# The first batch of a fused four-layer kernel in plain fp32: its products without splits, its small weights kept raw

## The chip, the cores and the metric

The kernel runs on one core of a Trainium2 chip. Its engines work side by side, each through its own queue in order: TensorE (PE, with its weight loads PEld), VectorE (DVE), ScalarE (ACT), GpSimd (POOL), and SyncE (SP), which issues transfers. The metric is the device time of one execution in microseconds; lower is better. Three executions of the kernel before took 2854.42, 2855.34 and 2858.27 us: the median is 2855.34.

## The reference

Sixteen sequences (batches) of 256 positions by 256 features go through four layers, each added to its input:

```
x = x + L0(x)     # traces: 16 decaying sums per sequence, gated, then layernorm
x = x + L1(x)     # masked softmax pooling over the sequence
x = x + L2(x)     # 8 experts and a shared one, 256 -> 1024 -> 256, all of them, weighted
x = x + L3(x)     # 256 -> 1024 -> 256, a part of the output weights chosen per sequence
```

What the change touches is L0 and L1 of the first sequence. In short:

```
ctx = scan(x, decay_ctx)
h1  = gelu(x @ Wn1);  mod = 0.5 + sigmoid(h1 @ Wn2)          # 16 rows, one per decay
g   = x * sigmoid([x, ctx] @ Wg)
temporal = sum over d of blend[d] * scan(g * mod[d], decay[d])
out = (gelu(x @ Wsoma) * sigmoid(temporal @ Wtemp)) @ Wout;  x1 = x + layernorm(out)
s   = tanh(x1 @ W1) @ v;  p = softmax(mask(s));  x2 = x1 + (p @ x1) / count
```

## The kernel before, in words

[...] So the kernel splits each operand in a rounded and a low part: `rnd` (L86) makes the rounded one, mostly on ScalarE (L88), `low` (L94) subtracts it from the original on VectorE or GpSimd (L95), and `mm3` (L100) makes a product of three passes: L101 high by high, L102 high by low, L103 low by high. Weights are split too: the small ones of L0 and L1 into `wh` and `wl` (`split_small`, L130), the expert weights chunk by chunk into a ring of ten tiles (`load_chunk`, L523), from two raw buffers. A raw buffer is free for the next transfer when both halves of its split are done.

Two generators give the work of one batch in steps: `traces(b, fast)` (L247) for the front of L0 and the decay loop, `pooled(b, fast)` (L392) for the rest of L0 and for L1. `fast` is true for batch 0 alone, which has nothing to hide behind: it uses two PSUM banks for most of its products, works in halves, and in its decay loop broadcasts the modulation by TensorE (L330), scales it on ScalarE (L335), multiplies on GpSimd (L338), scans on VectorE (L341), and sums with the identity on TensorE (L344). That last product is in plain fp32. The other batches send their modulation through DRAM and broadcast it by DMA (L354).

The order comes from the program's text, from a scheduler that fills each engine's queue by its own estimate of times, and from `tc.issue_after(...)`, which holds instructions behind a given one. First the constants are loaded (L137 to L154, on SP's and ScalarE's queues) and worked out (L160 to L224). Then 13 steps of batch 0's traces run (`FIRST`, L803), then pooled of batch 0 mixed with the first `FRONT` = 4 steps of batch 1's traces (L759), and the first expert chunks are fetched meanwhile (`prefetch`). From then on a plan of expert units (`l2_unit`, L620: products pg, pu, then y) and last-layer units (`l3_chunk`, L663) runs on TensorE, and the steps of batches 1 to 15 are spread between them at a pace set by due times.

Of the kernel before, what the change touches and what calls it, by code (L numbers as in the profile page):

```python
# [8 lines left out]
F32 = mybir.dt.float32  # L9
F32R = mybir.dt.float32r  # L10
# [6 lines left out]
NB = 16  # L17
# [6 lines left out]
FRONT = 4  # L24
SLACK = 16
# [19 lines left out]
def fused_kernel(  # L45
# [77 lines left out]
    small = {}  # L123

    def load_small(c0, c1, tag):
        raw = l0.tile([P, 512], F32, tag=tag, name=f"raw_{c0}", bufs=L0_BUFS.get(tag, 1))
        nc.sync.dma_start(raw[:, : c1 - c0], wsmall[:, c0:c1])
        small[c0] = raw[:, : c1 - c0]

    def split_small(c0, e):  # L130
        raw = small.pop(c0)
        c1 = c0 + raw.shape[1]
        rnd("a", wh[:, c0:c1], raw)
        low(e, wl[:, c0:c1], raw, wh[:, c0:c1])
# [4 lines left out]
    load_small(O_N1, O_N1 + 256, "bt")  # L139
    bl = const([P, 2, ND], F32, "bl", blend)  # L140
    load_small(O_G, O_G + 512, "tr")
    vec = const([P, V_COLS], F32, "vec", vecs)
    pti = const([P, NB], I32, "pti", ptype.partition_broadcast(P))
    sgt = const([P, NB], F32, "sgt", sgate.partition_broadcast(P))
    gat = const([P, NB, NE], F32, "gat", gates.partition_broadcast(P))
    load_small(O_G + 512, O_G + 1024, "tr")
    load_small(O_SO, O_SO + 512, "xo")
    load_small(O_TE, O_TE + 512, "sc")
    load_small(O_OU, O_OU + 512, "x1")
    load_small(O_W1, O_W1 + 256, "mb")  # L150
# [3 lines left out]
    eix = const([1, NB], I32, "eix", eidx, nc.sync)  # L154
    coef = cp.tile([P, NB, NE + 1], F32, name="coef")
# [7 lines left out]
    V.reciprocal(alpha, alpha)  # L163

    decay = ps_l.tile([P, ND + 1], F32, tag="decay", name="decay")
    V.tensor_copy(decay, alpha)
# [13 lines left out]
    vr = cp.tile([P, 2], F32R, name="vr")  # L180
    V.tensor_copy(vr[:, 0:1], vec[:, V_V : V_V + 1])
    low("v", vr[:, 1:2], vec[:, V_V : V_V + 1], vr[:, 0:1])
    n2 = cp.tile([P, 2, 48], F32R, name="n2")
    V.tensor_copy(n2[:, 0, :], vec[:, V_WN2 : V_WN2 + 48])
    low("v", n2[:, 1, :], vec[:, V_WN2 : V_WN2 + 48], n2[:, 0, :])

# [3 lines left out]

    jrow = cp.tile([P, 2], I32, name="jrow")
    G.iota(jrow, [[P, 2]], base=1, channel_multiplier=1)
    cnt = cp.tile([P, 3, 2], F32, name="cnt")
    V.tensor_copy(cnt[:, 0], jrow)
    V.tensor_scalar(cnt[:, 1], cnt[:, 0], -1.0, S + 1.0, ALU.mult, ALU.add)
    V.memset(cnt[:, 2], S - 1.0)
    flag = cp.tile([P, 3, NB], F32, name="flag")
    ptf = cp.tile([P, NB], F32, name="ptf")
    V.tensor_copy(ptf, pti)
    V.tensor_scalar(flag[:, 0], ptf, 0.0, None, ALU.is_equal)  # L200
    V.tensor_scalar(flag[:, 1], ptf, 1.0, None, ALU.is_equal)
    V.tensor_tensor(flag[:, 2], flag[:, 0], flag[:, 1], ALU.add)
    V.tensor_scalar(flag[:, 2], flag[:, 2], -1.0, 1.0, ALU.mult, ALU.add)

    kindf = cp.tile([P, NB], F32, name="kindf")
    V.tensor_scalar(kindf, flag[:, 0], -2.0, 2.0, ALU.mult, ALU.add)
    V.tensor_tensor(kindf, kindf, flag[:, 1], ALU.subtract)
    kind_i = cp.tile([P, NB], I32, name="kind_i")
    V.tensor_copy(kind_i, kindf)
    cntb = cp.tile([P, NB, 2], F32, name="cntb")  # L210
    ctmp = cp.tile([P, NB, 2], F32, name="ctmp")
    for t in range(3):
        o = cntb if t == 0 else ctmp
        V.tensor_tensor(
            o,
            flag[:, t].unsqueeze(2).to_broadcast([P, NB, 2]),
            cnt[:, t].unsqueeze(1).to_broadcast([P, NB, 2]),
            ALU.mult,
        )
        if t:  # L220
            V.tensor_tensor(cntb, cntb, ctmp, ALU.add)
    mhalf = cp.tile([P, 2], F32, name="mhalf")
    G.memset(mhalf, -0.5)
    bias3 = cp.tile([P, NB], F32, name="bias3")  # L224

# [21 lines left out]
    def traces(b, fast):  # L247
# [3 lines left out]
        rnd("v" if fast else "a", xh, xr)  # L251
        low("v" if fast else "g", xl, xr, xh)
        cx = ft("ta", f"ctx{b}")
        for c in range(2):
            last_of["cx"] = V.tensor_tensor_scan(
                cx[:, c], decay[:, ND : ND + 1].to_broadcast([P, S]), xr[:, c], 0.0, ALU.mult, ALU.add
            )
        yield
        if fast:
            split_small(O_N1, "v")  # L260
# [8 lines left out]
        if fast:  # L269
            with tc.issue_after(last_of["cx"].ins):  # L270
                split_small(O_G, "v")
                split_small(O_G + 512, "v")

                V.tensor_copy(coef[:, :, NE], sgt)
                V.tensor_scalar(sgt, sgt, -1.0, 1.0, ALU.mult, ALU.add)
                V.tensor_tensor(coef[:, :, 0:NE], gat, sgt.unsqueeze(2).to_broadcast([P, NB, NE]), ALU.mult)
# [12 lines left out]
        if fast:  # L289
            ms = l0.tile([48, S], F32R, tag="ths", name=f"ms{b}")  # L290
            rnd("v", ms, md)
            low("v", ms[32:], md[32:], ms[32:])
        else:
            mdd = dram.tile([1, ND, S], F32, tag="mdd", name=f"mdd{b}")
            nc.sync.dma_start(mdd[0], md[0:ND])
        yield
        pg = banks(fast, f"pg{b}")

        ga = ft("ga", f"ga{b}") if fast else ps_a.tile([P, 2, S], F32, tag="ga", name=f"gp{b}")
        for m in range(2):  # L300
            for k in range(4):
                o = O_G + k * S + m * P
                xa, xb_ = (xh[:, k], xl[:, k]) if k < 2 else (ch[:, k - 2], cl[:, k - 2])
                mm3(pg(m), W(0, o, P), W(1, o, P), xa, xb_, k == 0, k == 3)
        for m in range(2):
            A.activation(ga[:, m], pg(m), AF.Tanh, bias=hb[:, V_BG + m : V_BG + m + 1], scale=0.5)
        for c in halves(fast):
            V.scalar_tensor_tensor(ga[:, c], ga[:, c], 1.0, xr[:, c], ALU.add, ALU.mult)
# [12 lines left out]
        if fast:  # L321
            split_small(O_SO, "g")
            split_small(O_TE, "g")

            tacc = ps_y.tile([P, 2, S], F32, tag="y0", name=f"ta{b}")
            for d in range(ND):
                if d % 2 == 0:
                    pb = ps_gu.tile([P, 2, S], F32, tag="gu", name=f"pb{b}_{d}")
                    for i in range(2):
                        PE.matmul(  # L330
                            pb[:, i], sel[:, d + i : d + i + 1].to_broadcast([48, P]), ms, start=True, stop=True
                        )
                mod = l0.tile([P, 2, S], F32, tag="mod", name=f"mod{b}_{d}", bufs=2)
                for c in range(2):
                    last_of["a"] = A.activation(mod[:, c], pb[:, d % 2], AF.Copy, scale=bl[:, c, d : d + 1])  # L335
                bt = ft("bt", f"bt{b}_{d}", 3)
                e = "g" if d else "v"
                last_of[e] = (V if e == "v" else G).tensor_tensor(bt, ga, mod, ALU.mult)  # L338
                tr = ft("tr", f"tr{b}_{d}", 3)
                for c in range(2):  # L340
                    V.tensor_tensor_scan(  # L341
                        tr[:, c], decay[:, d : d + 1].to_broadcast([P, S]), bt[:, c], 0.0, ALU.mult, ALU.add
                    )
                PE.matmul(tacc, ident, tr, start=d == 0, stop=d == ND - 1)  # L344
                if d == 5:
                    soma()
                if d % 2:
                    yield
        else:
            tacc = ft("ta", f"ta{b}")  # L350
            for d in range(ND):
                if d % 2 == 0:
                    mod = l0.tile([P, 2, S], F32, tag="mod", name=f"mod{b}_{d}", bufs=2)
                    nc.sync.dma_start(mod, mdd[0, d : d + 2].partition_broadcast(P))  # L354
                bt = ft("bt", f"bt{b}_{d}", 3)
                tr = tacc if d == 0 else ft("tr", f"tr{b}_{d}", 3)
                with tc.issue_after(last_of[0].ins) if b == 1 and "h" not in last_of else nullcontext():
                    for c in range(2):
                        V.scalar_tensor_tensor(
                            bt[:, c], ga[:, c], bl[:, c, d : d + 1], mod[:, d % 2], ALU.mult, ALU.mult  # L360
                        )
                for c in range(2):
                    V.tensor_tensor_scan(  # L363
                        tr[:, c], decay[:, d : d + 1].to_broadcast([P, S]), bt[:, c], 0.0, ALU.mult, ALU.add
                    )
                if d:
                    G.tensor_tensor(tacc, tacc, tr, ALU.add)  # L367
                if d == 5:
                    soma()
                yield  # L370
# [602 lines left out]
```

## Time and profile before

One profiled execution of the kernel before:

| what | value |
|---|---|
| profiled execution's own time | 2854.52 us |
| its span on the core | 2852.3 us |
| mean granted TensorE clock | 0.993 |
| PE busy (matmuls) | 2781.6 us, 98% of the span |
| DVE busy | 1442.2 us, 51% |
| ACT busy | 1239.2 us, 43% |
| POOL busy | 1295.4 us, 45% |
| PE busy from 0 to 10 us | 1.89 us |
| PE busy from 50 to 60 us | 5.04 us |
| PE busy from 200 to 400 us | 179.09 us |
| PE busy from 400 to 800 us | 398.74 us |

The span is what the profiler saw on the core; the execution's own time also has what lies around it. Busy shares are averages over the whole span, and the first 73 us are of another kind than the rest. The ends of matmuls are modelled, so a busy PE isn't PE at its peak. In rows of the timeline the first two numbers are start and duration in us; the brackets hold the idle time before, and what ended it.

### The profile page before, as it was taken

What the parts mean: (1) busy time and instruction counts of PE and PEld (TensorE: products, weight loads), DVE (VectorE), ACT (ScalarE), POOL (GpSimd) and SP (SyncE); (2) the same over time, 40 slices, a digit from 0 to 9 for tenths busy, and PEclk for the clock granted to TensorE, in tenths of its full rate; (3) what the DMA queues carried; (4) which work ended last, traced back from release to release, by engine and by line L of the source; (5) the groups of instructions that cost most, each with busy time, mean ns of one, the idle gap of its engine ahead of it and who ended that gap; (6) DMA issues with size and microseconds to landing.
All of it is one profiled execution on the core that took longest, in us unless ns stands there. A gap on an engine that the chain in (4) does not pass through costs nothing. (4 is left out here: it accounts for less than half of the span.)

```text
span 2852.3 us, 36958 instructions
## 1 busy us (share of the span) xinstructions
PE 2781.6 (98%) x13632; PEld 2339.8 (82%) x13632; DVE 1442.2 (51%) x2661; ACT 1239.2 (43%) x2054; POOL 1295.4 (45%) x984
## 2 busy tenths in 40 slices
PE   6889889999999999999999999999999999999999
PEld 4887778888888888888888888888888888888887
DVE  7978866665665454444544445444444542222222
ACT  5565544456444533435334443344433453233433
POOL 4755544544645453543534445344454443333333
PEclk8999999999999999999999999999999999999999
DMA  3444546547443532323433143332523242222552
GB/s 106 132 144 137 162 149 217 176 144 244 149 159 120 172 123 100 118 80 92 173 105 125 40 167 117 107 118 66 181 100 110 93 159 98 89 89 76 189 196 86
DMA packets 114694, 371.24 MB, mean 130 GB/s; under 512 B 12642, under 2 KB 30930, under 8 KB 114514
## 3 DMA queue, kind: packets, MB, share of 16 engines
q1 hardware_dynamic: 113650, 368.74, 39.0%
q8 instruction: 108, 1.77, 0.3%
q14 instruction: 72, 0.59, 0.1%
q10 hardware_dynamic: 864, 0.14, 0.0%
HBM read 304.62 MB, written 64.21 MB: 129 GB/s over the span
## 5 line engine op out<-in xcount | busy, mean ns | idle before, releaser
L95 POOL TENSOR_TENSOR hh<-h,hh 128x512 fp32r<-128x512 f32 x640 | 848.4, 1326 | 1327.1 <-ACT hh L88 1307.4
L608 DVE TENSOR_TENSOR h<-h,pu 128x512 f32<-128x512 f32 x576 | 393.9, 684 | 939.6 <-PE pu L103 818.1
L88 ACT ACTIVATE hh<-h 128x512 fp32r<-128x512 f32 x640 | 403.5, 631 | 932.6 <-DVE h L608 912.4
L101 PE MATMUL pg<-x,w_e 128*128 128x512 f32 (+1 forms) x1232 | 467.3, 379 | 12.7 <-ACT x L88 5.4
L607 ACT ACTIVATE h<-pg 128x512 f32<-128x512 f32 x576 | 342.9, 595 | 306.6 <-PE pg L103 228.5
L101 PE MATMUL pu<-x,w_e 128*128 128x512 f32 (+1 forms) x1232 | 465.4, 378 | 6.5 <-ACT h L607 3.7
L103 PE MATMUL pg<-x,w_e 128*128 128x512 f32 (+1 forms) x1232 | 465.7, 378 | 4.2 <-DVE w_e L95 3.4
L102 PE MATMUL y<-hh,w_e 128*128 128x512 f32 (+1 forms) x1232 | 464.4, 377 | 3.2 <-POOL hh L95 3.2
L102 PE MATMUL pg<-x,w_e 128*128 128x512 f32 (+1 forms) x1232 | 465.3, 378 | 0.0
L103 PE MATMUL pu<-x,w_e 128*128 128x512 f32 (+1 forms) x1232 | 463.8, 376 | 0.0
L102 PE MATMUL pu<-x,w_e 128*128 128x512 f32 (+1 forms) x1232 | 463.6, 376 | 0.0
L103 PE MATMUL y<-hh,w_e 128*128 128x512 f32 (+1 forms) x1232 | 463.5, 377 | 0.0
L101 PE MATMUL y<-hh,w_e 128*128 128x512 f32 (+1 forms) x1232 | 415.6, 377 | 1.0 <-DVE acc L655 0.8
L367 POOL TENSOR_TENSOR ta<-ta,tr 128x512 f32<-128x512 f32 x225 | 308.4, 1371 | 67.6 <-DVE tr L363 53.9
L363 DVE TENSOR_TENSOR_SCAN tr<-decay,bt 128x256 f32<-128x256 f32 x450 | 285.1, 672 | 0.0
L101 PEld LDWEIGHTS pg<-x,w_e 128*128 128x128 f32 x1232 | 232.5, 189 | 56.4 <-ACT w_e L88 6.4
L101 PEld LDWEIGHTS pu<-x,w_e 128*128 128x128 f32 x1232 | 232.1, 188 | 50.5 <-ACT h L607 5.8
L103 PEld LDWEIGHTS pg<-x,w_e 128*128 128x128 f32 x1232 | 232.7, 189 | 47.8 <-DVE w_e L95 5.2
L102 PEld LDWEIGHTS y<-hh,w_e 128*128 128x128 f32 x1232 | 233.0, 189 | 47.0 <-POOL hh L95 5.5
L101 PEld LDWEIGHTS y<-hh,w_e 128*128 128x128 f32 x1232 | 231.5, 189 | 44.8 <-ACT hh L88 1.3
L103 PEld LDWEIGHTS y<-hh,w_e 128*128 128x128 f32 x1232 | 233.0, 189 | 41.7
L103 PEld LDWEIGHTS pu<-x,w_e 128*128 128x128 f32 x1232 | 232.3, 189 | 41.9
(294 smaller groups left out, 3267.5 us busy)
## 6 DMA issues: line engine op xcount, KB each, us to landing
w_e<-keep_e SPq DMA_DIRECT2D x216, 768.0 KB, 4.4
raw_e<-in_wexp_dram SPq DMA_DIRECT2D x144, 384.0 KB, 4.5
keep_e<-w_e SPq DMA_DIRECT2D x72, 768.0 KB, 4.2
mod<-mdd SPq DMA_DIRECT2D x120, 256.0 KB, 3.5
w_f<-keep_f SPq DMA_DIRECT2D x56, 384.0 KB, 3.6
raw_c<-in_comb_dram SPq DMA_DIRECT2D x32, 260.0 KB, 2.8
xr<-in_xT_dram SPq DMA_DIRECT2D x16, 256.0 KB, 3.1
xt<-in_x_dram SPq DMA_DIRECT2D x16, 256.0 KB, 2.7
```

The source lines that it names most:

```text
L88: last_of["ca"] = A.activation(out_, in_, AF.Copy)
L95: i = (V if e == "v" else G).tensor_tensor(out_, in_, h.bitcast(F32), ALU.subtract)
L101: PE.matmul(o, wh, xh, start=start, stop=False, **kw)
L102: PE.matmul(o, wh, xl, start=False, stop=False, **kw)
L103: last_of["pe"] = PE.matmul(o, wl, xh, start=False, stop=stop, **kw)
L363: V.tensor_tensor_scan(tr[:, c], decay[:, d : d + 1].to_broadcast([P, S]), bt[:, c], 0.0, ALU.mult, ALU.add)
L367: G.tensor_tensor(tacc, tacc, tr, ALU.add)
L607: A.activation(h, ps_g, AF.Silu)
L608: last_of["h"] = V.tensor_tensor(h, h, ps_u, ALU.mult)
```

## The change

Batch 0 gets generators of its own, `first_traces` and `first_pooled`; `traces` and `pooled` lose their `fast` branches. In the new ones every product but the broadcast of the modulation takes its operands as they are, in fp32, as one `PE.matmul` in place of `mm3`: no operand of batch 0 is rounded and no low part is made. Results in PSUM are brought to SBUF by `evict`, first half on ScalarE, second half on VectorE. The gate products of x (k = 0, 1) are issued ahead of those of ctx (k = 2, 3), soma's products come inside the decay loop, and soma's result `sm` lies in PSUM.

The small weights of batch 0 stay raw in two borrowed tiles (`raw_a` from the pool of x2, `raw_b` from that of acc). The splits, which the other batches need, come later in the text: three groups after the 13 steps with their low part on GpSimd, four by the table `rest` in batch 1's decay loop. In the instruction order that the scheduler makes of it, those four stand early again: on ScalarE between hg and md of batch 0, on GpSimd ahead of the decay loop; the three stand behind the decay loop, ahead of the first two expert chunks.

ScalarE's queue issues only the decays, the blend and the vectors; the types, the shared gate and the gates go to SP's queue. The reciprocal of the decays is written to PSUM at once. The constants that only later steps need are worked out after the first scans (`later_constants`, inside the hold of cx), the coefficients after batch 0 (`coefs`). The steps of batch 1 that are mixed with pooled of batch 0 are `FRONT0` = 3 instead of 4: the gate products of batch 1 come behind.

```diff
+FRONT0 = 3
...
+    raw_a = xs.tile([P, 2048], F32, tag="x2", name="small_a")
+    raw_b = accp.tile([P, 1024], F32, tag="acc", name="small_b")
...
+    def load_small(c0, c1):
+        nc.sync.dma_start(small(c0, c1 - c0), wsmall[:, c0:c1])
...
-    pti = const([P, NB], I32, "pti", ptype.partition_broadcast(P))
-    sgt = const([P, NB], F32, "sgt", sgate.partition_broadcast(P))
-    gat = const([P, NB, NE], F32, "gat", gates.partition_broadcast(P))
...
+    pti = const([P, NB], I32, "pti", ptype.partition_broadcast(P), nc.sync)
...
+    sgt = const([P, NB], F32, "sgt", sgate.partition_broadcast(P), nc.sync)
+    gat = const([P, NB, NE], F32, "gat", gates.partition_broadcast(P), nc.sync)
...
-    V.reciprocal(alpha, alpha)
...
-    V.tensor_copy(decay, alpha)
+    V.reciprocal(decay, alpha)
...
+    rest = {1: (O_SO, 512), 6: (O_TE, 512), 9: (O_OU, 512), 12: (O_W1, 256)}
...
+            if b == 1 and d in rest:
+                split_small(*rest[d], "g")
...
+    def evict(c, o, i):
+
+        if c == 0:
+            last_of["ca"] = A.activation(o, i, AF.Copy)
+        else:
+            last_of["cv"] = V.tensor_copy(o, i)
+
+    def first_traces():
...
+        for k in range(2):
+            PE.matmul(ph[:, :S], small(O_N1 + k * P, P), xr[:, k], start=k == 0, stop=k == 1)
...
+        gates_of((0, 1))
+        yield
...
+        last_of["pm"] = PE.matmul(pm[:48, :S], vec[0:64, V_WN2 : V_WN2 + 48], hg[0:64], start=True, stop=True)
...
+        with tc.issue_after(last_of["pm"].ins):
+            gates_of((2, 3))
...
+        sm = ps_a.tile([P, 2, S], F32, tag="ga", name="sm0")
...
+    def first_pooled():
...
+                PE.matmul(pt[m], small(O_TE + k * S + m * P, P), tt[:, k], start=k == 0, stop=k == 1)
...
+        for c in range(2):
+            last_of["cv"] = V.scalar_tensor_tensor(sg[:, c], sg[:, c], 1.0, sm[:, c], ALU.add, ALU.mult)
...
+        x1T = ft("xo", "x1T0")
+        for c in range(2):
+            evict(c, x1T[:, c], ptr[c])
...
+        q = ft("bt", "q0", 3)
+        for l in range(2):
+            evict(l, q[:, l], ppt[l])
...
+            front = FRONT if b else FRONT0
...
     while n_steps[0] < FIRST:
         next(steps)
+        if n_steps[0] == 4:
+            with tc.issue_after(last_of["cx"].ins):
+                later_constants()
+    with tc.issue_after(last_of["a"].ins), tc.issue_after(last_of["g"].ins), tc.issue_after(last_of["tr"].ins):
+        for off, n in ((O_N1, 256), (O_G, 512), (O_G + 512, 512)):
+            split_small(off, n, "g")
         prefetch(2, 0)
...
     with tc.issue_after(last_of["ca"].ins), tc.issue_after(last_of["cv"].ins):
+        coefs()
         prefetch(RING - n)
```

## The prediction

> **What bounds the kernel now.** I read the busy row in 40 slices first, then a table of stretches, then each engine's timeline up to the first matmul of the expert stage.
>
> ```profile
> PE   6889889999999999999999999999999999999999
> ...
> 30.00:40.00 10.00, 9.79 (x23) 3.64 (x23) 10.00 (x18) 7.27 (x18) 10.00 (x9) 1.00 0.00 1
> ...
> 60.00:70.00 10.00, 6.47 (x32) 5.66 (x30) 5.18 (x15) 4.44 (x10) 1.50 (x1) 0.59 0.58 189
> ...
> 100.00:110.00 10.00, 8.21 (x54) 7.80 (x53) 10.00 (x21) 3.85 (x6) 9.87 (x7) 0.83 0.50 144
> ...
> 800.00:1600.00 800.00, 800.00 (x3788) 671.61 (x3788) 401.83 (x771) 336.47 (x558) 371.30 (x289) 1.00 0.36 122
> ```
>
> The columns after a stretch are its length and the busy time of PE, PE's weight loads, DVE, ACT and POOL. From 400 us on TensorE never rests: nothing there can be won by a shorter wait. The gap is at the front. From 30 to 40 us POOL and DVE are full and PE does bookkeeping; from 60 to 70 us no engine is full: that is one batch going from engine to engine. Then, at 100 us, DVE and POOL are full again, with batch 1's traces and the splitting of expert weights.
>
> ```profile
> 8.11 0.58 PE L101 MATMUL ph<-x,wh 128*128 128x256 f32 x1 [8.11 <-DVE kindf L207]
> ...
> 48.05 0.58 PE L427 MATMUL po0g<-wh,s 128*128 128x256 f32 x1 [2.44 <-ACT s L88]
> ...
> 55.12 0.47 PE L447 MATMUL ptr0g<-ident,x 128*128 128x128 f32 x1 [3.43 <-DVE x L441]
> ...
> 62.25 0.55 PE L467 MATMUL psc<-ths,vr 128*128 128x256 f32 x1 [1.93 <-DVE ths L95]
> ...
> 68.70 0.27 PE L493 MATMUL ppt0g<-ident,sc 128*128 128x128 f32 x1
> ...
> 72.81 0.38 PE L101 MATMUL pg<-x,w_e 128*128 128x256 f32 x1 [0.73 <-ACT x L88]
> ```
>
> Each row is start, duration, operation, and in brackets the idle time before and who ended it. The first expert matmul is at 72.81 us. Everything the change touches lies before that, so the question is how far that row moves, and how much is still there at 400 us.
>
> **Until the trace loop.** Batch 0's loop over 16 decays is POOL's:
>
> ```profile
> 22.14 18.44 POOL L338 TENSOR_TENSOR bt<-ga,mod 128x512 f32<-128x512 f32 x15 [4.97 <-ACT mod L335]
> ...
> 6.12 1.28 ACT L161 ACT_TABLE_LOAD   x1 [6.12 <-DMA bl<-in_blend_dram]
> ...
> 12.05 0.63 ACT L88 ACTIVATE wh<-raw 128x512 fp32r<-128x512 f32 x1 [2.43 <-DMA raw<-in_wsmall_dram]
> ...
> 27.93 0.19 PEld L344 LDWEIGHTS ta<-tr,ident 128*128 128x128 f32 x1 [0.24 <-issue]
> 28.36 0.19 PEld L344 LDWEIGHTS ta<-tr,ident 128*128 128x128 f32 x1 [0.24 <-issue]
> ```
>
> Its 15 products take 18.44 us, 1.23 each, and are not changed; what counts is when the first starts (22.14). In the changed program's order:
> - ScalarE issues three DMAs, so its table load runs at about 2.1 to 3.4 instead of 6.12 behind two more issues. taub lands at 4.9 (0.74 + 4.2), bl at 5.5. DVE's order is reduce, subtract, alpha, reciprocal, reduce, scan: at 0.17 to 0.26 each the scans (0.69 + 0.61) run from 6.4 to 7.7; before, from 9.35 to 11.6. Some twenty index constants follow them, 0.1 each, done by 10.
> - TensorE needs no split: it starts at 5.9, when the first weights land (1.20 + 4.6). An fp32 product is not in this stage before, but the nearest row is: L344 multiplies 512 fp32 columns, has 32 records for 16 calls, and its loads follow 0.43 apart. So 512 columns cost 0.86 and 256 cost 0.43 warm, 0.85 cold, against 0.12 warm and 0.21 cold for one pass of the split form (the pitch of its rows at 18.3 and at 9.0: after a pause TensorE runs at half pace, and rows here come to 0.12 some 3 to 5 us into work). ph takes 5.9 to 7.6; four gate products take 2.9 (cold, warm from about 10) to 10.5; pm to 10.9; the last four to 12.6.
> - The four splits of the other small weights now stand in ScalarE's queue **between hg and md0**. They wait for landings: the third weight group's at 12.05 before, the last at 13.4 (issued 6.90, 6.5 to landing). So md0, whose operand is ready at 10.9, and both ga behind it wait: md0 13.3 to 13.8, ga to 14.6. Nothing hides this; if those landings come early (gates and sgate no longer ahead on ScalarE's queue), md0 is at 11.1.
> - md, ms and its low part on DVE (0.28, 0.28, 0.41), ga (0.85), then pb, mod (0.84), bt (0.69), mod again: POOL's first product at 17.1. POOL's own four low parts (1.28 each, the last half) end at 15.9. Here a rule speaks against the change: by the Trainium skill's "SBUF — State Buffer", section "SBUF: two separate sides", VectorE and GpSimd share a port pair as a lock and the loser waits out the whole instruction. The trace agrees (a cast at 60.30 took 1.35 beside a POOL product, the one at 18.35, as wide, 0.28). By the rule md and ms wait up to 1.3; by unblocked rows nothing. I take 0.5: start at 17.6.
> - Soma now sits after three mod steps: four fp32 products cold (3.4, from 16.2) and two activations hold mod 3 to about 20.4 and POOL some 0.9.
> Sum: 22.14 − 17.6 − 0.9 = **3.6 us** earlier at the loop's end; with bounds 2 (every lock lost) and 7 (landings early).
>
> **From the loop's end to the expert stage**, on the old clock, loop end at 40.58.
> - Five splits on the path go (round on ScalarE, low part on DVE, of t, s, u, ths and q). Where a PSUM tile must still be moved, one copy comes, half on each engine (0.38, 0.42).
> - t ready at 43.95 (before 44.8); four fp32 products, warm: 45.3; the gate's activations to 45.85.
> - The DVE product with soma, in halves:
>
> ```profile
> 45.92 1.63 DVE L413 SCALAR_TENSOR_TENSOR g<-g,sm 128x256 f32<-128x256 f32 x1
> ```
>
> This half took 1.63, the other 0.41: POOL was splitting. With sm in PSUM I take 0.45 each: done at 46.4. po is four products at 0.43, to 47.7; before 51.3.
>
> - POOL is a new bound here. Behind the loop stand now xt + beta (1.28), three weight lows (0.65, 1.28, 1.28), two expert chunks (1.78 each) and batch 1's x (1.25), then the power rs: 40.58 + 9.3 = 49.9, plus 0.7 for itself. DVE has rs ready at 49.2, so 0.7 is lost. x1 at 51.5; before 55.46: 3.9 won.
> - The same POOL queue holds the two raw buffers, so expert chunks 2 and 3 are requested at 46.9 and 48.7 instead of 42.4 and 44.1, and land 3.8 later. Their roundings sit in ScalarE's queue ahead of the copy of x1T: it is done at 54.1 though ptr was at 52.2. pa (two fp32, cold, 1.7), tanh, psc (0.85), reduction: 57.6, before 63.21.
> - Exponential and normalisation as before: 60.05 (before 65.70). The transposes no longer wait for batch 1's 24 gate products (64.04 to 68.84), which go behind the expert stage's start: 60.7. q's copies stand behind chunks 4 and 5: 62.3. pp cold: 64.9. First expert matmul **65.1**, before 72.81: 7.7 won. Bounds: 4 (all of ScalarE's and DVE's copies behind one more chunk, 3.5) and 9.
>
> By a second rule, the skill's "FP8 and Floating Point Precision", section "TensorE Precision Notes", true fp32 takes four passes where the split form takes three. The row says the same of 512 columns (0.86 against 0.235), and 30 products then cost 30 x 0.07 = 2.1 us more warm, 30 x 0.21 = 6.3 cold. By the rule alone this change loses; the waits ahead of the products in the rows above (2.44, 3.43, 1.93) are larger, and I have priced every product in fp32.
>
> **Behind 72.81.** Batch 1's 24 products (0.12 each, 2.9 us), its ga (0.69 on DVE) and the coefficient products (0.5 to 1.7) now come after the start; its trace begins some 3 us later against the expert stage. TensorE idles 3.0 us in the waits at 99.29 (1.23), 103.47 (1.29) and 104.48 (0.50), behind weight splits, so the 2.9 can go there; but DVE is full from 80 to 110 and passes on what it is given. Between 0 and 4 lost; I take 2. The later order, unit by unit, is the same with batch 1's steps about one unit later. The added splits' DMAs are the same transfers.
>
> Sum: 3.6 + 7.7 − 2.0 = **9.3 us**. The profiled execution took 2854.52 (span 2852.3), 0.8 below the median of 2855.34; so 2845.2 by its own time and **2846** as median.
>
> **Rivals.**
> - *Landings come early.* md0 at 11.1 wins 2.5 more, no lock lost, and the 2.9 disappears in idle: 13 to 16, 2841. For: gates' 64 KB leave the front. Against: nothing shows that they delayed the third group.
> - *Supply takes the wait's place.* The expert stage starts early but the chunks, requested 4.6 later on the loop's clock, and the full DVE decide at 100 us; of 11.3 only 2 to 5 are left: 2852, within 0.2% (5.7 us, what a measurement of this kernel can tell from no change). For: ScalarE waits 17.6 us for expert DMAs between 73 and 140. Against: chunks 6 and 7 keep their distance from the start (3.5 us after it, before 3.8).
> - *Slower: fp32 weight loads lie open.* If each record of the 26 fp32 products on the path also pays its load (0.19 warm, 0.33 cold), twice, at the cold clock, the path grows by 26 x 0.66 = 17 us, so 8 lost: 2863. It decides from 0.36 per product; slower by 0.2% needs 0.58. Against: L344's loads (0.19) fit inside 0.43.
> - *The change doesn't do what it says*: the built order has no split on batch 0's path, so no chance for it.
>
> **Numbers.** Forecast 0.50 (its own range 2842 to 2850), early landings 0.20, supply 0.19, open loads 0.11. Faster by over 0.2%: 0.70; within: 0.20; slower: 0.10. Range 2837 to 2860, which takes in the bounds.
>
> **What would show it.** First expert matmul at 59 to 64 us; POOL's loop from 17 to 19; ScalarE idle before a split ahead of md0; power rs waiting on POOL; fp32 records 0.43 apart warm. Wrong if the expert stage starts early and TensorE's waits between 73 and 200 (some 14 us) grow as much.

## The result and the profile after

The changed kernel takes 2841.99 us (median of six executions, 2841.67 to 2842.82); beside it the kernel before took 2854.88 (six, 2852.84 to 2858.44). The ratio is 0.9953, 95% interval 0.9941 to 0.9965: about 12.9 us faster by the medians, 0.47% by the ratio. The spans of the two profiled executions say 12.1: 2852.3 before, 2840.2 after, at nearly the same mean granted clock (0.993 and 0.994).

The same four stretches of the kernel after (columns: length, then busy time and instruction count of PE, PE's weight loads, DVE, ACT, POOL, then the granted clock, the DMA share and GB/s):

```profile
30.00:40.00 10.00, 8.89 (x21) 3.22 (x20) 6.75 (x12) 6.12 (x13) 10.00 (x10) 1.00 0.01 2
60.00:70.00 10.00, 10.00 (x86) 10.00 (x86) 5.72 (x9) 6.47 (x11) 5.13 (x3) 1.00 0.50 159
100.00:110.00 10.00, 8.72 (x68) 8.10 (x67) 10.00 (x20) 4.88 (x7) 9.84 (x7) 1.00 0.35 107
800.00:1600.00 800.00, 799.54 (x3778) 670.31 (x3778) 400.07 (x771) 335.80 (x559) 370.06 (x288) 1.00 0.35 116
```

From 60 to 70 us PE is now full at a clock of 1.00, where it was busy 6.47 of 10 at 0.59: the expert stage has begun. From 800 to 1600 us PE is as full as it was (799.5 of 800, before 800.0). At 100 us DVE and POOL are full as they were.

TensorE's timeline of the kernel after: the rows that answer to those of before, and the ends of what stands ahead of two of them:

```profile
5.93 2.05 PE L488 MATMUL ph<-xr,small_a 128*128 128x256 f32 x4 [5.93 <-DMA small_a<-in_wsmall_dram]
...
40.56 0.70 PE L583 MATMUL po0g<-small_b,g 128*128 128x256 f32 x2 [0.59 <-DVE g L574]
...
41.96 0.59 PE L583 MATMUL po0u<-small_b,g 128*128 128x256 f32 x2
...
45.52 0.33 PE L602 MATMUL ptr0g<-ident,x 128*128 128x128 f32 x1 [0.47 <-DVE x L594]
...
47.40 2.11 PE L609 MATMUL pa<-x1T,small_a 128*128 128x256 f32 x4 [1.04 <-ACT x1T L474]
...
50.07 1.22 PE L614 MATMUL psc<-th,vec 64*128 64x256 f32 x2 [0.56 <-ACT th L611]
...
53.24 0.48 PE L636 MATMUL ppt0g<-ident,sc 128*128 128x128 f32 x1 [0.42 <-DVE sc L631]
...
58.90 0.38 PE L102 MATMUL pg<-x,w_e 128*128 128x256 f32 x1 [0.53 <-ACT x L89]
```

The first expert matmul is at 58.90 instead of 72.81: **13.9 us earlier**, of which 12.1 are left at the end of the profiled execution.

The brackets alone mislead here: they count only the idle time since the instruction just before, and products of batch 1 stand in some of these stretches. What batch 0 waits is the time from the end of one of its products to the start of the next. For that, the last products of po, pa and psc in the kernel before:

```profile
50.99 0.34 PE L429 MATMUL po0u<-wh,s 128*128 128x256 f32 x1
...
57.97 0.42 PE L103 MATMUL pa<-u,wl 128*128 128x256 f32 x1
...
62.60 0.42 PE L468 MATMUL psc<-ths,vr 128*128 128x256 f32 x1
```

| from the end of | to the start of | before, us | after, us | what lies between |
|---|---|---|---|---|
| pt | po | 2.44 | 0.59 | gate, product with soma; before also the split of s |
| po | ptr | 3.79 | 2.97 | layernorm |
| pa | psc | 3.86 | 0.56 | tanh; before also the split of th |
| psc | ppt | 5.68 | 1.95 | softmax; before also batch 1's gate products |

These four give 9.7 us. The wait ahead of ptr, 3.43 in its bracket before and 0.47 after, was for the layernorm and not for a split: of it only 0.8 went.

The other engines' timelines of the kernel after:

```profile
10.46 2.51 POOL L96 TENSOR_TENSOR wl<-small_b,wh 128x512 fp32r<-128x512 f32 x2
...
16.53 18.49 POOL L533 TENSOR_TENSOR bt<-ga,mod 128x512 f32<-128x512 f32 x15 [2.83 <-ACT mod L530]
...
2.13 1.28 ACT L166 ACT_TABLE_LOAD   x1 [2.13 <-issue]
...
10.22 0.63 ACT L89 ACTIVATE wh<-small_b 128x512 fp32r<-128x512 f32 x1 [0.69 <-DMA small_b<-in_wsmall_dram]
...
11.36 0.47 ACT L504 ACTIVATE md<-pm,hb 48x256 f32<-48x256 f32 x1 [0.17 <-PE pm L502]
...
11.86 1.26 DVE L505 TENSOR_SCALAR md<-md 48x256 f32<-48x256 f32 x1
13.15 0.70 DVE L91 CAST ms<-md 48x256 fp32r<-48x256 f32 x1
...
40.09 0.85 DVE L574 SCALAR_TENSOR_TENSOR g<-g,sm 128x256 f32<-128x256 f32 x2 [1.70 <-ACT g L571]
...
44.24 0.70 POOL L589 TENSOR_TENSOR rs<-rs,mhalf 128x2 f32<-128x2 f32 x1
```

POOL's loop begins at 16.53 (before 22.14) and takes 18.49 us (18.44), so it ends 5.56 earlier, at 35.02. The four splits stand ahead of md0, as the prediction said, but only one waited for a landing, 0.69 us: md0 runs at 11.36, as soon as pm is done. md and ms take 1.26 and 0.70 on VectorE where the rows of before, beside an idle POOL, take 0.28: here POOL was splitting weights (from 10.46 to 12.97, and on to 13.70).

Where the 13.9 come from, in two stretches: the loop's end is 5.56 earlier, and from the loop's end to the first expert matmul it takes 23.88 instead of 32.23, 8.35 less. That is the 9.7 of the table less 1.3: po's products are 1.3 shorter, pp's 1.3 longer, and the other products and copies together 1.3 longer.

### The profile page after: what moved, and what is told of

The parts are those of the page before. It is cut to its first block, busy times and chain, and to the rows that moved or that the text cites. A ratio compares the mean times of both kernels' runs of the same rounds, so it can differ in the third digit from the quotient of the medians.

```text
span 2840.2 us, 36878 instructions
## 1 busy us (share of the span) xinstructions
PE 2779.2 (98%) x13604; PEld 2335.0 (82%) x13604; DVE 1425.2 (50%) x2646; ACT 1235.4 (43%) x2043; POOL 1299.0 (46%) x986
```

## The experiments

"Start" is the first expert matmul of the profiled execution, "rest" the span from there to the end. A difference of medians of a few us is at the edge of what can be told: the ratios' intervals reach some 3 to 5 us to either side. Where a verdict rests on less, the trace decides it or it stays open.

| run | median, us | ratio to before, 95% | start | rest |
|---|---|---|---|---|
| before | 2854.88 | | 72.81 | 2779.5 |
| after | 2841.99 | 0.9953 [0.9941, 0.9965] | 58.90 | 2781.3 |
| e1 constants back on ScalarE's queue | 2843.57 | 0.9961 [0.9947, 0.9975] | 65.27 | 2780.7 |
| e2 gates ahead of the third weights | 2843.52 | 0.996 [0.9946, 0.9974] | 61.20 | 2778.2 |
| e3 sm in SBUF | 2845.64 | 0.9968 [0.9955, 0.998] | 64.11 | 2780.1 |
| e4 batch 1's gates in front | 2849.11 | 0.9978 [0.9969, 0.9988] | 62.93 | 2783.6 |
| e5 before, with the queue part alone | 2854.02 | 0.9995 [0.9986, 1.0004] | 72.74 | 2779.7 |
| e6 chunks 2 and 3 fetched earlier | 2841.34 | 0.9952 [0.9935, 0.9968] | 58.79 | 2779.6 |
| e9 TensorE kept at pace | 2842.61 | 0.9957 [0.994, 0.9973] | 56.81 | 2783.0 |
| e10 e9 and e6 | 2841.93 | 0.9954 [0.9938, 0.9971] | 56.71 | 2782.9 |
| e11 nine ring tiles | 2848.8 | 0.9975 [0.9965, 0.9985] | 58.98 | 2787.9 |
| e12 e11 with three raw buffers | 2850.24 | 0.9981 [0.9972, 0.9991] | 58.85 | 2792.9 |
| e13 e10 with nine tiles, three buffers | 2845.36 | 0.9963 [0.9949, 0.9977] | 56.70 | 2785.3 |

### e1: the constants' transfers back on ScalarE's queue

```diff
-    pti = const([P, NB], I32, "pti", ptype.partition_broadcast(P), nc.sync)
+    pti = const([P, NB], I32, "pti", ptype.partition_broadcast(P))
+    sgt = const([P, NB], F32, "sgt", sgate.partition_broadcast(P))
+    gat = const([P, NB, NE], F32, "gat", gates.partition_broadcast(P))
...
-    sgt = const([P, NB], F32, "sgt", sgate.partition_broadcast(P), nc.sync)
-    gat = const([P, NB, NE], F32, "gat", gates.partition_broadcast(P), nc.sync)
```

> The changed kernel with its types, shared gate and gates loaded on ScalarE's queue again, behind the vectors. It separates the queue part from the fp32 part. Theory (the three broadcasts held both ScalarE's first table load and the landing of the later weight groups): the table load starts after 6 us instead of 2.1, the last raw weight group lands at 13 instead of 10.8, md of batch 0 starts at 13.3 or later instead of 11.4, POOL's loop starts at 18.3 or later instead of 16.5, and the first expert matmul moves from 58.9 to 60.7 or later: 1.8 to 3 us slower than the changed kernel, some 2844 to 2845. Rival (the landings came early only because their requests went out 0.4 to 0.6 us sooner on SP's queue): md starts before 12 and the first expert matmul before 59.6.

ScalarE's timeline of this run:

```profile
6.22 1.28 ACT L166 ACT_TABLE_LOAD   x1 [6.22 <-DMA bl<-in_blend_dram]
...
13.38 1.31 ACT L89 ACTIVATE wh<-small_b 128x512 fp32r<-128x512 f32 x2 [3.23 <-DMA small_b<-in_wsmall_dram]
14.90 0.45 ACT L504 ACTIVATE md<-pm,hb 48x256 f32<-48x256 f32 x1
```

Soma's products on TensorE, in the kernel after and then in this run:

```profile
15.24 1.99 PE L546 MATMUL pso<-xr,small_a 128*128 128x256 f32 x8
```

```profile
19.72 3.78 PE L546 MATMUL pso<-xr,small_a 128*128 128x256 f32 x8
```

Here is the stall that the prediction had put into the changed kernel: a split waits 3.23 us for its landing, and md0, queued behind it, runs at 14.90 instead of 11.36. The table load is back at 6.22. POOL's loop starts at 20.62, 4.1 later, and stalls 2.20 after two products: ScalarE waits for soma, whose four products take 3.78 us at a granted clock of 0.50 (18 to 24 us), after TensorE had paused for 4.52. In the kernel after the pause was 1.11, the clock 1.00, and they took 1.99. The expert stage starts at 65.27, 6.4 later, well beyond what had been expected: 4.1 by the late loop and 2.2 by that stall. The profiled execution was 5.8 longer, but it is the slowest of this run's five; the median is 1.6 longer, within the intervals. What the queue part is worth at the start is shown; how much of it reaches the end isn't.

### e2: the gates' transfers alone, ahead of the third weights

```diff
     pti = const([P, NB], I32, "pti", ptype.partition_broadcast(P), nc.sync)
+    sgt = const([P, NB], F32, "sgt", sgate.partition_broadcast(P), nc.sync)
+    gat = const([P, NB, NE], F32, "gat", gates.partition_broadcast(P), nc.sync)
     load_small(O_SO, O_SO + 512)
...
-    sgt = const([P, NB], F32, "sgt", sgate.partition_broadcast(P), nc.sync)
-    gat = const([P, NB, NE], F32, "gat", gates.partition_broadcast(P), nc.sync)
```

> The changed kernel with shared gate and gates on SP's queue, but right behind the types, so ahead of the third group of small weights; ScalarE's queue stays clean. It tells the landings apart from the table load. If the 64 KB of gates in front delay the weights, the table load stays at 2.1 but the last weight group lands 1 us or more later than 10.8 and md starts at 12 or later. If they don't, md starts at 11.4 to 11.7 and the time is within 1 us of the changed kernel, 2841 to 2843.

ScalarE's timeline:

```profile
10.84 0.63 ACT L89 ACTIVATE wh<-small_a 128x512 fp32r<-128x512 f32 x1 [2.30 <-DMA small_a<-in_wsmall_dram]
...
12.05 0.45 ACT L504 ACTIVATE md<-pm,hb 48x256 f32<-48x256 f32 x1
```

The first of these splits ran at 8.39 in the kernel after; with the shared gate and the gates' 64 KB ahead it waits 2.30 for its landing and runs at 10.84. So they do hold back the weights behind them; 0.9 of it is the later request (5.86 instead of 4.96). md0 itself is only 0.7 later, with two splits ahead of it here and two behind. The loop starts 1.4 later and stalls 0.93 for soma, whose products took 2.91 (granted clock 0.50 from 18 to 20 us, after a pause of 2.08). The start is 2.3 later; the time can't be told from the kernel after.

### e3: soma's result in SBUF instead of PSUM

```diff
-        sm = ps_a.tile([P, 2, S], F32, tag="ga", name="sm0")
+        sm = ft("sm", "sm0")
```

> The changed kernel with soma's result sm in SBUF instead of PSUM, nothing else. Theory (a VectorE operation with two SBUF operands waits while POOL works on SBUF): the product of gate and soma, 0.85 us for two halves in the changed kernel beside POOL's splits, takes 1.6 to 2.5, and the first expert matmul comes 0.8 to 1.7 later than 58.9. Rival (no lock there, the slow half in the kernel before was an accident of the schedule): 0.85 again, and no difference of the first expert matmul beyond 0.2.

The summary of VectorE's product with sm in this run, its durations as min/median/max in ns; it was issued at 40.05:

```profile
L574 DVE SCALAR_TENSOR_TENSOR g<-g,sm x2: 413/2364/4314, 40.0 to 44.3; 128x256 f32<-128x256 f32 x2
```

And POOL's timeline in the same run:

```profile
39.30 3.55 POOL L96 TENSOR_TENSOR w_e<-raw_e,w_e 128x768 fp32r<-128x768 f32 x2
42.83 1.25 POOL L96 TENSOR_TENSOR x<-xr,x 128x512 fp32r<-128x512 f32 x1
```

The first half took 4.31 us, the other 0.41; with sm in PSUM each takes 0.43. It began while POOL was on its first chunk, and was done at 44.36, 0.3 after POOL's last instruction of that row ended (44.08). One chunk takes 1.78, so waiting for one instruction would have ended by 41.1. The wait was for **POOL's whole unbroken row**: larger than either theory had it. It is one instruction in one execution, but the half that was slow in the kernel before fits it. That one began at 45.92, took 1.63, and POOL's row there was:

```profile
44.08 1.96 POOL L95 TENSOR_TENSOR wl<-raw,wh 128x512 fp32r<-128x512 f32 x2
46.01 1.25 POOL L95 TENSOR_TENSOR x<-xr,x 128x512 fp32r<-128x512 f32 x1
```

The instruction that it met was done at 46.04; it ended at 47.55, 0.3 after the end of the next one (47.26). In e3 the start moves by 5.2: 3.9 by this wait and 1.8 by po's four products, which behind a pause of 4.48 took 3.79 instead of 1.99 (granted clock 0.50 from 44 to 48 us), less some 0.5 that came back in the layernorm. The time moves by 3.65.

### e4: batch 1's gate products in front again

```diff
-FRONT0 = 3
+FRONT0 = 4
```

> The changed kernel with FRONT0 = 4, so that batch 1's 24 gate products are mixed with pooled of batch 0 again. It prices the move of these products behind the start of the expert stage. Theory (they stood on batch 0's path, between its reductions and its transposes): the first expert matmul comes 2 to 3.5 later than 58.9, at 61 to 62.5, and the time behind it gets shorter by up to as much, since that work is done: 2841 to 2844. Rival (with shorter products the gates find a place in TensorE's pauses): first expert matmul at 58.9 to 59.5, and the time at or below that of the changed kernel.

The 24 products of batch 1 stand between psc and ppt once more: ppt is at 59.06 (after: 53.24). They keep TensorE at pace, so pp runs at 0.43 a product instead of 0.85, and the start is 4.0 later. Nothing comes back behind it: the rest is longer by another 2.3, the time by 7.1, and here the interval lies clear of that of the kernel after. So, by the time, the order of batch 1's gates is the largest single part of the gain that was measured by undoing it. That the time behind the start would get shorter, as expected, did not come true. Why the rest grows too wasn't traced.

### e5: the queue part alone, on the kernel before

```diff
-    pti = const([P, NB], I32, "pti", ptype.partition_broadcast(P))
-    sgt = const([P, NB], F32, "sgt", sgate.partition_broadcast(P))
-    gat = const([P, NB, NE], F32, "gat", gates.partition_broadcast(P))
+    pti = const([P, NB], I32, "pti", ptype.partition_broadcast(P), nc.sync)
...
+    sgt = const([P, NB], F32, "sgt", sgate.partition_broadcast(P), nc.sync)
+    gat = const([P, NB, NE], F32, "gat", gates.partition_broadcast(P), nc.sync)
```

> The kernel before with the queue part of the change alone: types, shared gate and gates on SP's queue (the last two at its end), everything else as it was, splits included. Theory (the fp32 form carries nearly all): batch 0's first part gains what the table load and the landings give, POOL's loop starts 1 to 3 us earlier than 22.1, and the time falls by 1 to 3 us from the kernel before, to some 2852 to 2854. Rival (the queue part carries half or more): 6 us or more, POOL's loop from 17 or less, 2849 or less.

POOL's loop begins 2.3 us earlier than before (19.86) and ends 1.3 later (41.86). The table of stretches in this run, with the granted clock in the third column from the right:

```profile
18.00:22.00 4.00, 2.01 (x9) 1.24 (x8) 2.80 (x5) 3.24 (x8) 2.14 (x2) 0.78 0.12 46
22.00:26.00 4.00, 4.00 (x7) 1.55 (x6) 3.86 (x7) 2.51 (x6) 4.00 (x5) 0.50 0.01 2
26.00:30.00 4.00, 4.00 (x6) 1.24 (x5) 2.10 (x4) 2.52 (x6) 3.28 (x4) 0.50 0.01 2
30.00:34.00 4.00, 4.00 (x6) 1.46 (x6) 2.11 (x5) 1.68 (x4) 2.10 (x3) 0.51 0.00 0
34.00:38.00 4.00, 4.00 (x12) 1.77 (x12) 3.69 (x7) 1.68 (x4) 3.25 (x3) 1.00 0.01 2
```

And TensorE's timeline in it:

```profile
25.57 3.78 PE L344 MATMUL ta<-tr,ident 128*128 128x512 f32 x4
30.01 3.78 PE L344 MATMUL ta<-tr,ident 128*128 128x512 f32 x4
34.24 1.98 PE L344 MATMUL ta<-tr,ident 128*128 128x512 f32 x4
```

For 12 us TensorE has half its clock, a pair of sums takes 3.78 instead of 1.98, and from 26 us on VectorE and POOL, which were the bound of this loop, drop towards half busy: TensorE is the bound until its clock returns at 34. In the kernel before the three stretches from 22 us on have 0.73, 0.85 and 1.00, in the kernel after all have 1.00. The 1 to 3 us that were expected of this run are not there. So the queue part is worth 6.4 us at the start with the fp32 products (e1) and nothing without: the parts of this change don't add. The likely reason: in the kernel after, the fp32 gate and soma products stand from 5.9 us up to the loop's first sum at 17.90 with no pause above 1.11, and TensorE comes into the loop at 1.00. e1 and e2 fit this: with a pause of 4.52 and of 2.08 ahead of soma their clock was 0.50 at 18 to 20 us. No run changes the pauses alone, and why the clock stays at 0.50 for 12 us in e5 isn't known.

### e6: expert chunks 2 and 3 fetched ahead of the three splits

```diff
+        prefetch(2, 0)
         for off, n in ((O_N1, 256), (O_G, 512), (O_G + 512, 512)):
             split_small(off, n, "g")
-        prefetch(2, 0)
```

> The changed kernel with the first two expert chunks ahead of the three late splits of small weights, on ScalarE and POOL. It tests the rival of the prediction in which the supply of expert weights takes the wait's place: chunks 2 and 3 are requested 3.2 us earlier (near 38 instead of 41.2). If supply decides behind the start, the time falls by 2 us or more, to 2840 or less. If batch 0's path alone decides, the first expert matmul moves by 0.6 at most (one rounding less ahead of the copy of x1T) and the time stays within 1.5 us of 2842.

The two chunks are requested at 38.07 instead of 41.18. Start and time stay (58.79; 2841.34): the requests of the next four chunks are where they were, at 46.79 and 54.77. Nothing is won: the front is not waiting for chunks 2 and 3. On the supply of the later ones this run says nothing.

### e9 and e10: TensorE kept at its full pace

In the kernel after the granted clock is 0.50 from 48 to 56 us, and the tail's fp32 products stand 0.85 apart. In e9, 44 more products (14, 8, 6, 12 and 4 behind po, ptr, pa, psc and ppt) write to an unused bank of PSUM that nobody reads. e10 has e6's edit too.

```diff
+    def warm(n, after):
+        wt = ps_y.tile([P, 512], F32, tag="y1", name=f"warm{after.ins.name if hasattr(after.ins, 'name') else ''}"[:24])
+        with tc.issue_after(after.ins):
+            for _ in range(n):
+                PE.matmul(wt[:, :S], W(0, O_G, P), W(0, O_G, S), start=True, stop=True)
...
+        warm(14, pe)
```

> The changed kernel with 44 products of float32r on TensorE added that no one reads, in the pauses of pooled of batch 0 (14 behind po, 8 behind ptr, 6 behind pa, 12 behind psc, 4 behind ppt), into a PSUM bank that is free then. It tests how much of the fp32 products' price there is the half clock after pauses. Theory (pace follows recent work): pa, psc and pp go at 0.43 per 256 columns instead of 0.85, 7 products, so that the first expert matmul comes 1.5 to 3 earlier than 58.9. Rival (the added products are too few, or stand in the way): half pace stays, and the first expert matmul comes at 58.9 or up to 2 later.

> Both edits together: the unread products in TensorE's pauses and the first two expert chunks ahead of the three late splits. If both help and add, the first expert matmul is at 55.5 to 57 and the time some 2837 to 2840; if what is won at the front is absorbed behind it, the time stays at 2841 to 2843 although the expert stage starts earlier.

TensorE's timeline of e9:

```profile
47.77 1.44 PE L617 MATMUL pa<-x1T,small_a 128*128 128x256 f32 x4 [0.25 <-ACT x1T L474]
...
49.84 0.69 PE L623 MATMUL psc<-th,vec 64*128 64x256 f32 x2
...
54.28 0.70 PE L655 MATMUL pp0g<-q,x 128*128 128x256 f32 x2 [0.24 <-ACT q L474]
...
56.81 0.39 PE L102 MATMUL pg<-x,w_e 128*128 128x256 f32 x1 [0.53 <-ACT x L89]
```

The granted clock is 1.00 from 40 to 56 us. pa falls from 2.11 to 1.44, psc from 1.22 to 0.69, and the start is 2.1 earlier. The time is not: 2842.61, and 2841.93 in e10. Where the 2.1 went can be seen on ScalarE. First its timeline in the kernel after, then in e9:

```profile
59.18 1.57 ACT L89 ACTIVATE w_e<-raw_e 128x768 fp32r<-128x768 f32 x2
...
65.96 0.85 ACT L89 ACTIVATE w_e<-raw_e 128x768 fp32r<-128x768 f32 x1 [1.81 <-DMA raw_e<-in_wexp_dram]
```

```profile
59.04 0.85 ACT L89 ACTIVATE w_e<-raw_e 128x768 fp32r<-128x768 f32 x1 [1.06 <-DMA raw_e<-in_wexp_dram]
...
65.47 0.85 ACT L89 ACTIVATE w_e<-raw_e 128x768 fp32r<-128x768 f32 x1 [2.29 <-DMA raw_e<-in_wexp_dram]
```

By 65 us the lead is 0.5: ScalarE now waits for two chunks to land. The second of them, the ninth chunk, had been requested 2.0 earlier (60.91 instead of 62.92), so the lead was lost in the transfer: 4.6 us from the request to the split instead of 3.0. Two transfers of batch 1's modulation, 256 KB each, had been requested just ahead of it (from 59.21); that they are the reason isn't tested. This is the rival of the prediction in which supply takes the wait's place, at work on the last 2 us.

### e11 to e13: a third raw buffer

For a third raw buffer the ring has to give up a tile. e11 is the control; e12 adds the buffer; e13 adds it to e10.

```diff
-RING = 10
+RING = 9
...
-    raws = ctx.enter_context(tc.tile_pool(name="raws", bufs=2))
+    raws = ctx.enter_context(tc.tile_pool(name="raws", bufs=3))
```

> The changed kernel with nine ring tiles in place of ten, to make room for a third raw buffer in the next run; this one is its control. The first ten expert chunks are no longer all fetched ahead: the tenth waits for a tile. Expected: the first expert matmul where it was (58.9 us, within 0.5), the time 2842 to 2846. If the ring's depth carries the front, up to 2850.

> As the run before with three raw buffers in place of two (nine ring tiles). Theory, supply absorbs: behind the start the expert chunks wait for a raw buffer; with a third one chunk 2 is requested with the first two and the others 2 to 4 us earlier, and the time falls 2 to 4 us below that with two buffers. Rival, engines: VectorE and GpSimd, full from 75 to 120 us, decide; then the third buffer changes the time by under 1 us.

> As the run before (nine ring tiles, three raw buffers), with TensorE held at pace by unread products and chunks 2 and 3 asked for ahead of the splits. Theory, supply absorbs: the 2.1 us by which this brings the first expert matmul forward now reach the end, so it is 1.5 to 2.5 us below the run before. Rival, engines: it is the same within 1 us.

With nine tiles the start stays (58.98) and the time rises to 2848.8, more than the 2842 to 2846 expected (before was 1.2 slower beside these runs than beside the first ones). The third buffer alone brings nothing: 2850.24, although the ninth chunk is then split before 62 us instead of at 65.96. But with it the lead of the front arrives. SP's queue, requests of expert chunks, in e12 and then in e13:

```profile
63.29 1.28 SPq L673 DMA_DIRECT2D raw_e<-in_wexp_dram  x3
76.08 1.25 SPq L673 DMA_DIRECT2D raw_e<-in_wexp_dram  x2
...
101.31 37.72 SPq L673 DMA_DIRECT2D raw_e<-in_wexp_dram  x16
```

```profile
60.73 1.28 SPq L684 DMA_DIRECT2D raw_e<-in_wexp_dram  x3
73.67 1.25 SPq L684 DMA_DIRECT2D raw_e<-in_wexp_dram  x2
...
98.82 37.62 SPq L684 DMA_DIRECT2D raw_e<-in_wexp_dram  x16
```

The lead is 2.6, 2.4 and 2.5 us, still whole at 100 us. With two buffers e9's requests at the same places lead those of the kernel after by 0.5 (69.36 against 69.86, 99.86 against 100.37). e13's five executions (2843.85 to 2845.59) all lie below e12's ten (2847.08 to 2856.30); the medians differ by 4.9, more than the 2.1 of the start, and the intervals of the ratios still touch. So each theory had a part: with two buffers the chunks' supply swallows what the front wins beyond about 59 us, as e9's rows show; but a third buffer does not by itself make the expert stage faster. Between 58 and 140 us SP's requests still wait 37.4 us in e12 for VectorE's halves of the splits (32.2 in e11), which points to VectorE as the pace behind both. (e12's profiled execution was 3.4 us above its median, so its rest in the table is too long by about that.) None of these three beats the kernel after.

## Why the prediction was right, and where it wasn't

The direction was right, and so was most of the mechanism: the start comes earlier because waits go, and fp32 products cost less than that. The forecast (2846, own range 2842 to 2850) was 4 us too high; the measured 2841.99 lies at the edge of that range, nearer to the 2841 of early landings, which had been given only 0.20. Step by step:

- **Until the loop: 3.6 predicted, 5.56 measured.** The term that was mis-sized is the stall of md0. The prediction said that it and the gates behind it "wait: md0 13.3 to 13.8", since the third weight group had landed at 12.05 and the last at 13.4. In the kernel after the four splits ran from 8.39 to 11.19, and md0 at 11.36. The rival of early landings had named this (md0 at 11.1, 2841), and on the landings it was right; not on the rest, for the lock did cost time and time was lost behind the start. I had held against it that nothing shows that the gates delayed the third group. e2 shows that they do (2.5 us, 0.9 of it by the later request), and e1 that the stall is real where the transfers are as before. A landing time read in one order of transfers was carried over to another.
- **The lock was under-sized.** 0.5 was taken; md and ms lost 0.98 and 0.42, together 1.4, a little above the 1.3 that I had as the bound by the rule of the Trainium skill's "SBUF — State Buffer", section "SBUF: two separate sides", that the loser waits out one whole instruction. Here the rule holds: md was done 0.15 after the POOL instruction that it had met (12.97). In e3 it is too short: 3.9 us were lost by one instruction, which ended only after POOL's next two.
- **Soma's stall of 0.9 didn't occur.** The loop's 15 products stand in one row of 18.49. The four fp32 products had been taken as cold (3.4); at a granted clock of 1.00 they took 1.99. In e2, where they took 2.91, the stall is there, 0.93: the step was right for another clock. That lock and soma were off by as much in opposite ways is luck. Together: 1.9 too much for md0, 0.9 too little for the lock, 0.9 too much for soma, which is 1.9 net and the whole difference.
- **From the loop's end to the start: 7.7 predicted, 8.35 measured.** On the clock of the loop's end the product with soma (0.45 per half; 0.43), rs's wait on POOL (at 49.9; 49.8) and its 0.7 are as predicted. The copy of x1T was not held up by as much (pa at 53.0 instead of 54.1), the last transpose ended at 60.1 instead of 60.7, and pp began at 60.6 instead of 62.3, as it needed only the first of q's two copies (the second was done at 61.5). pp and what follows took 3.9 instead of 2.8: pp's four products were under-sized, 2.6 where at half clock they take 3.3. Moving batch 1's gates was in this sum; e4 gives it 4.0 of the start. Of the three waits that the prediction held against the price of fp32 (2.44, 3.43, 1.93), the second was the layernorm's and went by 0.8 only, and the third is part of a stretch from pa to psc that went by 3.3.
- **fp32 in place of the split form.** The products stood 0.43 apart warm (pt at 37.98, 38.52, 38.95 and 39.38) and 0.85 cold, as read from L344. Loads did not lie open, so the rival on the slower side (2863) falls. The rule of the Trainium skill's "FP8 and Floating Point Precision", section "TensorE Precision Notes", that true fp32 takes four passes, makes the product dearer than the split form's three, and the pace agrees (0.43 against 0.36 for three passes at 0.12). It didn't decide: the waits that went were larger.
- **Behind the start: 2.0 predicted to be lost, 1.8 measured** (13.9 less 12.1, each from one profiled execution; by the medians 1.0). That it is the same quantity isn't shown: I had put it on VectorE and batch 1's products, and e4, which moves those products to the front, makes the rest longer, not shorter. e9 points to the expert chunks' supply as what absorbs any further gain.

What stays open: what the fp32 form is worth by itself (no run puts the splits back into the kernel after; with the queue part, but without the move of the gates, it is some 6 us, e4), how much of e1's 6.4 us reaches the end, what keeps e5's clock at half, why e4 lengthens the rest, and why e13 gains 4.9 on e12 from 2.1 at the start.

## What to carry to other kernels

A landing time belongs to its queue order: when transfers are moved away from in front of others, work out the later landings anew before you price a stall on them. In a stretch where one item goes from engine to engine, count the time from the end of one of its products to the start of the next, not the products alone, and not the bracket, which other work can fill: a form that takes longer on an engine wins if it takes away a hand-over (here 3.3 us from pa to psc, against 0.45 more for psc). And before speeding up a front further, look at the queue that feeds the stage behind it: the last 2 us were won at the start and gone within 10 us.

## What the runs showed of the hardware that wasn't expected

- A VectorE instruction of two SBUF operands that meets a busy POOL can wait for more than the instruction in flight: 4.31 us instead of 0.41, until POOL's unbroken row ended (e3; the kernel before has a smaller case, 1.63 instead of 0.41). With one operand in PSUM it took 0.42 beside such a row in the kernel after. The 48x256 instructions with one operand, md and ms, lost time beside POOL too (1.26 and 0.70 for 0.28), and so did a cast of 16 columns (1.28 at 9.25 us, for 0.17 before); md was done 0.15 after the one POOL instruction that it met, while POOL's next still ran.
- A loop paced by VectorE and POOL can fall to half TensorE clock and stay there for 12 us although TensorE's records show it full (e5: 0.50 from 22 to 34 us). TensorE then becomes the bound that it wasn't. Pauses of 2.08 and 4.52 us ahead of the loop came with a clock of 0.50 behind them (e2, e1), one of 1.11 with 1.00.
- Some 44 unread products of 256 columns in the pauses held the tail at its full pace: granted clock 1.00 instead of 0.50, a psc of 0.69 instead of 1.22 (e9).
